# Cross attention's query and output projections as seven products of quarters instead of eight

## The chip, the cores and the metric

One core of a Trainium2 chip runs the whole program. The metric is device time in microseconds (us) of one launch. All data are fp32. TensorE (PE in the profile; PEld is its weight load) multiplies, VectorE (DVE), ScalarE (ACT) and GpSimd (POOL) work on elements, and SyncE (SP) issues every transfer. Each engine takes its instructions in the program's order; semaphores hold one back until what it needs is there.

## What is computed

One layer of an encoder over `ctx_1024` (2 x 77 x 512) and one of a decoder over `x` (2 x 2048 x 512), both with 16 heads of 32. The change touches the decoder's cross attention, the middle line, which reads the encoder's 77 rows:

```python
y = y + _mha(yn, yn, dec_sa_in_w, dec_sa_in_b, dec_sa_out_w, dec_sa_out_b, sb)
y = y + _mha(_ln(y, dec_n2_s, dec_n2_b), memory, dec_ca_in_w, dec_ca_in_b, dec_ca_out_w, dec_ca_out_b, cb)
h = _ln(y, dec_n3_s, dec_n3_b)
y = y + (jax.nn.relu(h @ dec_ff1_w.T + dec_ff1_b) @ dec_ff2_w.T + dec_ff2_b)
```

`_mha` projects queries, keys and values, adds a bias by relative position to the scaled scores, takes a softmax, weighs the values and projects the result.

## The kernel before

**Two halves.** The 4096 tokens of the decoder are eight blocks of 512 tokens, each of four tiles of 128. The first half of the program is the decoder's self-attention, as 128 units (block, group of four heads, tile of queries), 16 units to a block, with the encoder spread between them; the results go to DRAM as `y1`. Extra work hangs in lists by unit: `light[n]`, `jobs[n]`, `late[n]` run in this order at the start of unit n, `ahead[n]` just before (L1003 `slot`, L1463). The unit u is the first of a block. Every block computes, during the block before it, its norm (L277 `norm_stats`, whose power stands on POOL, L285; L288 `norm_center`, on VectorE), in units 6 to 9, where also the residual's bias is added on POOL (L266). Block 0's cross attention runs in the first half too (L833 `first_cross`).

**Sums of weights.** In blocks 2 and 6 of the first half, in units u, u + 2, u + 4 and u + 10, quarters of the feed-forward weights are loaded, combined on POOL (L1090 `w2_sums`, L1123 `w1_sums`; L1088 `minus` is the helper that all subtractions go through) and stored in DRAM.

**The second half** (from about 1756 us) is the feed-forward of blocks 0 to 7, with the cross attention of block x + 1 laid beside that of block x. The feed-forward's products are already done as seven products of quarters instead of eight, after Winograd: `ONE` and `TWO` (L1157, L1166) list for each of the seven the weights' part, the tokens' part, the chain (one of two accumulating banks) and the quarter of the result that the bank's content goes to after it. A block has 56 slots (L1362 `ff_slot`): 0 to 27 hold the first layer's products, four matmuls of 128 x 256 each (L1292 `first_product`, L1301); 28 to 55 the second layer's, seven products of four parts (L1321 `second_product`, L1330), three parts with eight matmuls of 128 x 128 and the fourth with four. Sums of tokens feed them:

- `sums_n` (L1223), all four on POOL in slot 0, 512 wide (L1088).
- `sums_h` (L1258), one product ahead, in slots 24 to 51: the half sums on VectorE (L1250 and L1088), the others on POOL (L1268, L1088) where the product's part is itself a sum, as it is in products 1 to 4, hence in slots 28 to 43.
- Evictions of second products: L1338 on ScalarE, L1339 and L1344 to L1346 on VectorE, and the addition to y on POOL (L1349).

Weights come as tiles of 256 KB through a ring of 16 (L1195 `w_ring`, L1198 `feed`), in the order in which the products take them.

**Cross attention** (L1384 `cross`): a generator that adds, ahead of each slot's own products, what `plan[slot]` lists.

- Norm n2 (L732 `norm_stages`): tile t has its statistics (VectorE, then a power and a product on POOL, L743 and L744) in slot t, its centering (ScalarE, L750) and the addition of a bias row to y (POOL, L751) in slot t + 2, its turning (four transposes on PE, L756, and four copies on ScalarE, L759) in slot t + 4.
- Queries (L763 `q_group`): four groups of features in slots 9 to 12, four matmuls of 128 x 512 each (L766), evicted on VectorE with bias and scale (L767).
- Attention per tile (L769 `attend_stages`), from slot 14, 21, 28 and 35: the scores (PE L781) with maximum and subtraction (VectorE L790, L791), the exponential (ScalarE L794), three slots later the row sums (VectorE L799, L800) and the division (POOL L805), then the turning of the probabilities (PE L811, ScalarE L812) after six, the values (PE L819, ScalarE L823) after nine, and the output (four matmuls of 128 x 512, L828, added to y on VectorE, L829) after eleven: slots 25, 32, 39 and 46. The first tile's scores stand one slot and its exponential, sums and division one slot or none earlier than this.
- Norm n3, whose turned result feeds the next block's first products: statistics, centering with addition, turning in slots 27, 29, 31 for tile 0 and 7 slots later for each further tile (48, 50, 52 for tile 3).

The side work uses four PSUM banks in turn (`bank`), the feed-forward the other four. The last block has nothing beside it.

Of the kernel before, what the change touches and what calls it, by code (L numbers as in the profile page):

```python
# [10 lines left out]
F32 = mybir.dt.float32  # L11
# [43 lines left out]
def tile_encoder_decoder(ctx: ExitStack, tc: tile.TileContext, ins, out):  # L55
# [5 lines left out]
    def wchunk(name, c0, n=D):  # L61

        return ins[name][:, c0 : c0 + n].rearrange("(c p) o -> p c o", p=P)
# [4 lines left out]
    ident = const.tile([P, P], F32, name="ident")  # L68
    make_identity(nc, ident)
    mhalf = const.tile([P, TB], F32, name="mhalf")  # L70
    nc.gpsimd.memset(mhalf, -0.5)
    vecs = const.tile([P, NVEC], F32, name="vecs")

# [84 lines left out]
    with (  # L158
# [573 lines left out]
        def norm_stages(y, n, row, place, done):  # L732

            keep = {}

            def stats():
                st = sm.tile([P, 6], F32, name="bnst", tag="bnst")
                mv = sm.tile([P, 2], F32, name="cmv", tag="cmv", bufs=4)
                rs = sm.tile([P, 3], F32, name="crs", tag="crs", bufs=4)
                nc.vector.bn_stats(st, y())  # L740
                nc.vector.bn_aggr(mv, st)
                nc.vector.tensor_scalar_add(rs[:, 0:1], mv[:, 1:2], EPS)
                nc.gpsimd.tensor_tensor(rs[:, 1:2], rs[:, 0:1], mhalf[:, 0:1], ALU.pow)  # L743
                nc.gpsimd.tensor_scalar(rs[:, 2:3], mv[:, 0:1], rs[:, 1:2], -1.0, ALU.mult, ALU.mult)  # L744
                keep.update(rs=rs)

            def center():
                xn = keep["xn"] = place()
                rs = keep["rs"]
                nc.scalar.activation(xn, y(), AF.Identity, bias=rs[:, 2:3], scale=rs[:, 1:2])  # L750
                nc.gpsimd.tensor_tensor(y(), y(), row, ALU.add)  # L751

            def turned():
                xn, pt, dst = keep["xn"], bank(), done()
                for c in range(NC):
                    nc.tensor.transpose(pt[:, ts(c, P)], xn[:, ts(c, P)], ident)  # L756
                for c in range(NC):
                    sc, bi = vec(f"dec_{n}_s", c), vec(f"dec_{n}_b", c)
                    nc.scalar.activation(dst[:, c, :], pt[:, ts(c, P)], AF.Identity, bias=bi, scale=sc)  # L759

            return stats, center, turned

        def q_group(o, w, nT, dst):  # L763
            mm = bank()
# [4 lines left out]
        def attend_stages(q, kTc, v, y, biased, pr, pts, place, w_o, bi=None):  # L769
# [58 lines left out]
                    nc.tensor.matmul(mm, oT[:, ts(c, P)], w_o[:, c, :], start=(c == 0), stop=(c == NC - 1))  # L828
                nc.vector.tensor_tensor(y(), mm, y(), ALU.add)  # L829

            return score, exp, sums, normalize, turned, times_v, out

        def first_cross():  # L833

# [40 lines left out]
            for t in range(TB):  # L875
                y = lambda t=t: ys[t]
                fs = norm_stages(
                    y, "n2", rows["dec_ca_out_b"], lambda: xn, lambda t=t: nT[:, :, ts(t, P)]
                )
                for k, f in enumerate(fs):  # L880
                    at(1 + t + k, f)
            for g in range(NC):
                at(7 + g, lambda g=g: q_group(g, wq[:, :, ts(g, P)], nT, qT[:, g, :]))
            for t in range(TB):
                y = lambda t=t: ys[t]
                fs = attend_stages(
                    lambda g, t=t: qT[:, g, ts(t, P)], kTc, vc, y, t < 2, prs[t % 2], pts, lambda: oT, wo
                )
# [3 lines left out]
                for k, f in enumerate(fs):  # L892
# [133 lines left out]
        w_q, vcs, qT = [], [], []  # L1026

        def big(i):
            return vflat[:, i * TB * D : (i + 1) * TB * D]
# [3 lines left out]
        def y_of(x, t):  # L1033
            return ys[x % 3][:, t, :]
# [6 lines left out]
        def early_loads():  # L1041
            nc.sync.dma_start(nTt, nT3_d)
            row_into(bv, "dec_ca_out_b")
            for o in range(2):
                w_q.append(small_w(o * P, "dec_ca_in_wT"))
            w_q.append(pts_all[:, 6, :].rearrange("p (c o) -> p c o", c=NC))

        def last_loads():
            t = sb.tile([P, MB], F32, name="q", tag="q", bufs=3)
            t = t.rearrange("p (c o) -> p c o", c=NC)  # L1050
            nc.sync.dma_start(t, wchunk("dec_ca_in_wT", (NC - 1) * P, P))
            w_q.append(t)
            for b in range(B):
                t = sb.tile([P, MB], F32, name="q", tag="q", bufs=3)
                nc.sync.dma_start(t[:S, :], cv_d[:, b, :])
                vcs.append(t)

        def late_loads():
            nc.sync.dma_start(w_q[2], wchunk("dec_ca_in_wT", 2 * P, P))
# [15 lines left out]

        w1_d = dram.tile([4, NC, P, D], F32, name="w1_d")
        w2_d = dram.tile([7, 7, P, D], F32, name="w2_d")
        free = pp[:, 3 * HC * MB : END - 3 * HC * MB]
        tens = free.rearrange("p (z q o) -> p z q o", z=8, q=2)
        ones = {  # L1080
# [55 lines left out]
        def w1_store(n):  # L1136
            nc.sync.dma_start(
                w1_d[:, n].rearrange("s p x -> p s x"), free[:, 4 * D :].rearrange("p (s x) -> p s x", s=4)
            )

        u = 2 * NU
        for c, k in enumerate((0, 2, 4, 10)):
            light[u + k + 2].append(lambda c=c: w2_store(c, 1))
# [36 lines left out]
        def w1_tile(name, n):  # L1180
# [3 lines left out]
            o = r * (DFF // 2) + n * TOK  # L1184
            return ins["dec_ff1_wT"][c * TOK : (c + 1) * TOK, o : o + TOK].rearrange("(c p) o -> p c o", p=P)

        def weight_tiles():
            for x in range(len(blocks)):
                for j, n in first_slots:
                    yield w1_tile(ONE[j][0], n)  # L1190
                for _, name, _, _, _ in TWO:
                    for k in range(7):
                        yield w2_d[ON_W2[name], k]
# [29 lines left out]
        def sums_n():  # L1223
            minus(gp, of_n("T1"), of_n("12"), of_n("11"))
            minus(gp, of_n("T2"), of_n("22"), of_n("T1"))
            minus(gp, of_n("T3"), of_n("22"), of_n("12"))
            minus(gp, of_n("T4"), of_n("21"), of_n("T2"))


        sets = [[high[:, (4 * a + k) * D : (4 * a + k + 1) * D] for k in range(4)] for a in range(2)]  # L1230
# [153 lines left out]
        def cross(x):  # L1384
# [162 lines left out]
```

## Time and profile before

| | us |
|---|---|
| median of three runs | 2870.43 |
| lowest and highest | 2868.46, 2870.47 |
| the profiled execution's span | 2868.2 |
| TensorE busy | 2821.6 |
| VectorE busy | 1930.3 |
| ScalarE busy | 1371.7 |
| POOL busy | 741.8 |

The profile has no other time of its own execution than the span; runs of this kernel lie up to 2.3 us above it. In the timeline a row merges neighbouring instructions of one kind: start, length from the first start to the last end, engine, line, operation, what is written and read, count, and in brackets the idle time ahead of it with what ended it. A matmul of the code stands as two instructions in the trace. Matmuls overlap, so their pace is read from start to start, not from one's length.

### The profile page before, as it was taken

Reading aid. Unit: us, or ns where it says so; the run is one execution under the profiler, and the core shown is the slowest. Engines: PE = TensorE matmul, PEld = TensorE weight load, DVE = VectorE, ACT = ScalarE, POOL = GpSimd, SP = SyncE. Lnnn points to the kernel's source line nnn. Section 1 sums busy time; section 2 is a strip of 40 time slices with the busy share of each in tenths; the row PEclk is TensorE's granted clock in tenths of the full one; section 3 lists DMA queues with packets and bytes.
Section 4 is the critical chain, followed back from the end, with each engine's and each line's share of the span. In section 5 each row is a group of like instructions: output and inputs, shape, how many; then the busy total and the mean of one; then the engine's idle time right before and its main releaser. Section 6 shows DMA issues by size and latency. Waiting matters only on the chain.

```text
span 2868.2 us, 64539 instructions
## 1 busy us (share of the span) xinstructions
PE 2821.6 (98%) x25782; PEld 2036.2 (71%) x25782; DVE 1930.3 (67%) x5422; ACT 1371.7 (48%) x2583; POOL 741.8 (26%) x637
## 2 busy tenths in 40 slices
PE   9899999999999999999999999999999999999998
PEld 5557666666666556666666677787878788888888
DVE  4767688778987668788878894555555555554545
ACT  3344455556666446565546665333333333333331
POOL 0100050200000201120100002272737373736355
PEclk9899999999999999999999999999999999999999
DMA  6413443401111512232301115464647464645365
GB/s 174 117 33 122 124 135 101 119 20 45 33 44 58 137 29 62 77 100 71 93 16 39 38 35 162 149 188 125 188 126 205 129 188 127 186 129 184 115 204 181
DMA packets 251773, 316.16 MB, mean 110 GB/s; under 512 B 29472, under 2 KB 142672, under 8 KB 251346
## 3 DMA queue, kind: packets, MB, share of 16 engines
q1 hardware_dynamic: 251474, 312.05, 36.7%
q8 instruction: 203, 3.33, 0.5%
q14 instruction: 96, 0.79, 0.1%
HBM read 273.07 MB, written 38.90 MB: 109 GB/s over the span
## 4 chain that ended last, share of the span: by engine, by line
PE 90%; DVE 3%; ACT 3%; POOL 2%; DMA 1%; issue 1%; SPq 0%; POOLq 0%; DVEq 0%; ACTq 0%
PE psum L425 17%; PE psum L1330 12%; PE psum L1301 11%; PE psum L371 11%; PE psum L442 9%; PE psum L828 4%; PE psum L766 4%; PE psum L215 4%; PE psum L239 4%; PE psum L251 4%; PE psum L226 3%; PE psum L811 2%; PE psum L781 1%; PE psum L819 1%; ACT pp L402 1%
## 5 line engine op out<-in xcount | busy, mean ns | idle before, releaser
L402 ACT ACTIVATE pp<-pp,nm 128x128 f32<-128x128 f32 (+15 forms) x512 | 611.9, 1201 | 263.2 <-DVE nm L397 262.9
L380 DVE TENSOR_SCALAR_CACHE_REDUCE pp<-psum 128x512 f32<-128x512 f32 (+3 forms) x1024 | 559.5, 591 | 62.1 <-PE psum L371 59.9
L425 PEld LDWEIGHTS psum<-ident,pp 128*128 128x128 f32 x4352 | 475.1, 142 | 110.5 <-DVE pp L380 50.8
L425 PE MATMUL psum<-ident,pp 128*128 128x128 f32 x4352 | 537.8, 278 | 8.5 <-DVE mx L387 3.8
L431 ACT COPY pts<-psum 128x512 f32<-128x512 f32 (+3 forms) x592 | 297.9, 575 | 470.9 <-PE psum L425 364.8
L429 DVE COPY pts<-psum 128x512 f32<-128x512 f32 (+2 forms) x544 | 329.9, 659 | 67.8 <-PE psum L425 67.5
L371 PE MATMUL psum<-kT,q 32*128 32x512 f32 (+3 forms) x2560 | 362.8, 578 | 5.9 <-ACT pts L431 3.3
L442 PEld LDWEIGHTS psum<-pts,vv 128*32 128x32 f32 x8704 | 227.3, 110 | 126.2 <-issue 117.3
L1330 PE MATMUL psum<-pp 128*128 128x128 f32 x2560 | 306.4, 276 | 1.9 <-POOL pp L1088 1.6
L1330 PEld LDWEIGHTS psum<-pp 128*128 128x128 f32 x2560 | 295.8, 192 | 17.4 <-issue 12.1
L442 PE MATMUL psum<-pts,vv 128*32 128x128 f32 x8704 | 280.9, 277 | 0.7 <-ACT pts L431 0.5
L1301 PE MATMUL psum<-vv,pp 128*128 128x256 f32 x1024 | 238.5, 381 | 0.0
L371 PEld LDWEIGHTS psum<-kT,q 32*128 32x128 f32 x2560 | 125.3, 184 | 143.3 <-issue 88.2
L1301 PEld LDWEIGHTS psum<-vv,pp 128*128 128x128 f32 x1024 | 189.8, 190 | 32.2 <-issue 8.4
L387 DVE CUSTOM_DVE_ANT_0 pp<-psum,bias 128x256 f32<-128x256 f32 (+1 forms) x512 | 196.0, 411 | 16.3 <-PE psum L371 16.3
L1088 POOL TENSOR_TENSOR pp<-pp 128x512 f32<-128x512 f32 x124 | 171.0, 1394 | 105.4 <-DMA pp<-in_dec_ff_wT_dram 91.2
L285 POOL TENSOR_TENSOR rstd<-rstd,mhalf 128x1 f32<-128x1 f32 x32 | 18.2, 570 | 662.8 <-DVE rstd L284 662.8
L1314 DVE TENSOR_TENSOR kT<-kT,psum 128x512 f32<-128x512 f32 x96 | 65.8, 686 | 170.3 <-PE psum L1301 96.9
L1317 ACT ACTIVATE kT<-kT,vecs 128x256 f32<-128x256 f32 x192 | 86.9, 500 | 192.0 <-DVE kT L1314 192.0
L1301 PE MATMUL psum<-nT,pp 128*128 128x256 f32 x768 | 173.4, 379 | 0.0
L1301 PEld LDWEIGHTS psum<-nT,pp 128*128 128x128 f32 x768 | 145.3, 190 | 28.6 <-issue 10.2
L805 POOL TENSOR_TENSOR oT<-oT,cri 128x1232 f32<-128x1232 f32 x28 | 67.7, 2419 | 346.2 <-DVE cri L800 346.2
(187 smaller groups left out, 3671.8 us busy)
## 6 DMA issues: line engine op xcount, KB each, us to landing
pp<-w_d SPq DMA_DIRECT2D x520, 256.0 KB, 3.0
pp<-in_dec_ff_wT_dram SPq DMA_DIRECT2D x112, 256.0 KB, 3.9
wqk<-in_dec_sa_in_wT_dram SPq DMA_DIRECT2D x64, 256.0 KB, 4.0
bias<-tzg SPq DMA_DIRECT2D x128, 128.0 KB, 3.8
wbig<-in_dec_sa_in_wT_dram SPq DMA_DIRECT2D x8, 1024.0 KB, 6.5
vv<-in_enc_ff_wT_dram SPq DMA_DIRECT2D x8, 1024.0 KB, 5.7
wbig<-in_dec_sa_out_wT_dram SPq DMA_DIRECT2D x8, 1024.0 KB, 6.4
vv<-y SPq DMA_DIRECT2D x32, 256.0 KB, 4.9
```

The source lines that it names most:

```text
L215: nc.tensor.matmul(mm, w[:, c, :], nTs[b, m][:, c, :], start=(c == 0), stop=(c == NC - 1))
L371: nc.tensor.matmul(banks[r][:, : kn * P], q[rows4(r), ts(t, P)], kT[rows4(r), g, k0 * P : (k0 + kn) * P], start=True, stop=True,)
L380: nc.vector.tensor_scalar(p[:, k0 * P : (k0 + far) * P], s[:, : far * P], 1.0, None, ALU.mult, ALU.max, accum_out=st["mx"][:, r, c : c + 1],)
L387: nc.vector.tensor_tensor_reduce(p[:, (i + 1) * P - w : (i + 1) * P], s[:, far * P : kn * P], biases[b, m, g][:, r, 2 * P - w :], 1.0, LOW ...
L402: nc.scalar.activation(p, p, AF.Exp, bias=nm, accum_out=to)
L425: nc.tensor.transpose(pt[:, ts(x, P)], state[n]["p"][r][:, ts(k, P)], ident)
L429: nc.vector.tensor_copy(pts[:, : len(load), :], pt[:, :w])
L431: nc.scalar.copy(pts[:, : len(load), :], pt[:, :w])
L442: nc.tensor.matmul(ot[rows4(r), t, :], vv[:, k, ts(g * HC + r, HD)], got.pop((n, k, r)), start=(k == 0), stop=(k == i),)
L1088: engine.tensor_tensor(out, a, b, ALU.subtract)
L1301: nc.tensor.matmul(mm[:, ts(f, TOK)], a[:, c, ts(f, P)], b[:, c, :], start=fresh and f == 0 and c == 0, stop=c == 1, skip_group_check=True,)
L1330: nc.tensor.matmul(psum[:, bank_i, ts(col, P)], lhs[:, c, :], w[:, c, :], start=fresh and k in (0, 3) and c == 0, stop=c == 3, skip_group_ ...
```

## The change

The query projection and, for pairs of tiles, the output projection become seven products of quarters each, with sums of weights made in the first half and streamed through the ring; the sums of tokens and some additions move. Both are done for the cross attentions of blocks 1 to 7; `first_cross` keeps its form (it uses the norm's new fourth stage).

- In units u + 7 of blocks 2 and 6 of the first half (u = 32 and 96), four loads and four POOL operations 512 wide make four weight sums, and a store in unit u + 8 puts them into DRAM.
- Query products: 0 and 1 in slot 9, 2 and 3 in slot 10, 4 and 5 in slot 11, 6 in slot 12, four matmuls of 128 x 256 each, on four token sums made on POOL in slots 8 and 9. First results of a quarter are evicted on ScalarE in two halves, later ones on VectorE.
- Output products: for tiles 0 and 1 in slots 31 to 33, for tiles 2 and 3 in slots 46 to 48, two matmuls of 128 x 256 each, on four sums made on VectorE, 256 wide, at the beginning of slots 31 and 46. Each product's bank is added to y on VectorE, 256 wide.
- Norm n2's addition to y goes from slot t + 2 to t + 11. Norm n3's statistics go to slots 35, 36, 49 and 50 for tiles 0 to 3, centering and addition two slots, turning four slots later.
- The four sums of `sums_n` go to slots 0, 1, 4 and 6, one each.

```diff
@@ norm_stages
                 nc.scalar.activation(xn, y(), AF.Identity, bias=rs[:, 2:3], scale=rs[:, 1:2])
+
+            def add():
                 nc.gpsimd.tensor_tensor(y(), y(), row, ALU.add)
...
-            return stats, center, turned
+            return stats, center, turned, add
@@ sums of weights
+        def wc_sums(name, turned):
+            z = free.rearrange("p (z k o) -> p z k o", z=8, k=2)
+            q = {}
+            for i, (r, c) in enumerate(((0, 0), (0, 1), (1, 0), (1, 1))):
+                nc.sync.dma_start(z[:, i], quarter(name, c, r) if turned else quarter(name, r, c))
+                q[r, c] = z[:, i]
+            s1, s2, s3, s4 = (z[:, 4 + i] for i in range(4))
+            if turned:
+                gp.tensor_tensor(s1, q[1, 0], q[1, 1], ALU.add)
+                minus(gp, s2, s1, q[0, 0])
...
+        for u, name, turned, dst in (
+            (2 * NU, "dec_ca_in_wT", True, wq_d), (6 * NU, "dec_ca_out_wT", False, wo_d)
+        ):
+            light[u + 7].append(lambda name=name, turned=turned: wc_sums(name, turned))
+            late[u + 8].append(lambda dst=dst: wc_store(dst))
@@ the ring's order
+        Q_SLOTS = {9: (0, 1), 10: (2, 3), 11: (4, 5), 12: (6,)}
+        O_SLOTS = {at + k: js for at in (31, 46) for k, js in enumerate(((0, 1), (2, 3), (4, 5, 6)))}
...
         def weight_tiles():
             for x in range(len(blocks)):
...
+                for n in range(per):
+                    if x + 1 < len(blocks):
+                        yield from cross_tiles(n)
@@ ff_slot
-            if n == 0:
-                sums_n()
+            if n in (0, 1, 4, 6):
+                sum_n(f"T{(0, 1, 4, 6).index(n) + 1}", of_n)
@@ cross
-                for k, f in zip((0, 2, 4), fs):
+                for k, f in zip((0, 2, 4, 11), fs):
                     plan[t + k].append(f)
-            for g in range(NC):
-                plan[9 + g].append(lambda g=g: q_group(g, w_q[g], nT2, qT[g // 2][:, g % 2, :]))
...
+            def q_product(j):
+                if j == 0:
+                    held["q"] = bank(), bank()
+                name, by, chain, fresh, to = ONE[j]
+                a, n, mm = next_w(2), of_n2(by), held["q"][chain]
+                for f in range(2):
+                    for c in range(2):
+                        nc.tensor.matmul(
+                            mm[:, ts(f, TOK)], a[:, c, ts(f, P)], n[:, c, :],
+                            start=fresh and f == 0 and c == 0, stop=c == 1, skip_group_check=True,
+                        )
+                r, c = int(to[0]) - 1, int(to[1]) - 1
+                got, dst = mm.rearrange("p (f n) -> p f n", f=2), qT[r][:, :, ts(c, TOK)]
+                if to in [p[4] for p in ONE[:j]]:
+                    nc.vector.scalar_tensor_tensor(dst, got, SCALE, dst, ALU.mult, ALU.add)
+                else:
+                    for f in range(2):
+                        nc.scalar.activation(
+                            dst[:, f, :], got[:, f, :], AF.Identity, bias=qbias[:, 2 * r + f : 2 * r + f + 1], scale=SCALE
+                        )
+
+            plan[8].append(lambda: [sum_n(n, of_n2) for n in ("T1", "T2")])
+            plan[9].append(lambda: [sum_n(n, of_n2) for n in ("T3", "T4")])
...
+            def sums_o(t):
+                s = {n: of_o(t, n) for n in ("S1", "S2", "S3", "S4", "11", "12", "21", "22")}
+                ve.tensor_tensor(s["S1"], s["21"], s["22"], ALU.add)
+                minus(ve, s["S2"], s["S1"], s["11"])
+                minus(ve, s["S3"], s["11"], s["21"])
+                minus(ve, s["S4"], s["12"], s["S2"])
+
+            def o_product(t, j):
+                if j == 0:
+                    held["out"] = bank(), bank()
+                name, by, chain, fresh, to = ONE[j]
+                a, mm = of_o(t, name), held["out"][chain][:, :TOK]
...
+                for c in range(2):
+                    nc.tensor.matmul(
+                        mm, a[:, ts(c, P)], w[:, c, :], start=fresh and c == 0, stop=c == 1, skip_group_check=True
+                    )
+                d = y_of(x, t + int(to[0]) - 1)[:, ts(int(to[1]) - 1, TOK)]
+                ve.tensor_tensor(d, d, mm, ALU.add)
+
+            for n, js in Q_SLOTS.items():
+                plan[n].append(lambda js=js: [q_product(j) for j in js])
+            for n, js in O_SLOTS.items():
+                t = 0 if n < 40 else 2
+                if 0 in js:
+                    plan[n].append(lambda t=t: sums_o(t))
+                plan[n].append(lambda t=t, js=js: [o_product(t, j) for j in js])
...
-                for k, f in zip((0, 2, 3, 3, 6, 9, 11) if t else (-1, 1, 2, 3, 6, 9, 11), fs):
+                for k, f in zip((0, 2, 3, 3, 6, 9) if t else (-1, 1, 2, 3, 6, 9), fs):
                     plan[at + k].append(f)
                 fs = norm_stages(y, "n3", bo, place("xt"), lambda t=t: nTt[:, :, ts(t, P)])
-                for k, f in zip((13, 15, 17), fs):
+                at = (35, 36, 49, 50)[t]
+                for k, f in zip((0, 2, 4, 2), fs):
                     plan[at + k].append(f)
```

More of the change, by code (lines that the diff above doesn't have):

```diff
@@ L70, in tile_encoder_decoder @@
     mhalf = const.tile([P, TB], F32, name="mhalf")
+    qbias = const.tile([P, NC], F32, name="qbias")
     nc.gpsimd.memset(mhalf, -0.5)
@@ L829, in out @@
                 nc.vector.tensor_tensor(y(), mm, y(), ALU.add)
-            return score, exp, sums, normalize, turned, times_v, out
+            return score, exp, sums, normalize, turned, times_v, out, keep
         def first_cross():
@@ L879, in first_cross @@
                 )
-                for k, f in enumerate(fs):
+                for k, f in zip((0, 1, 2, 1), fs):
                     at(1 + t + k, f)
@@ L1077, in tile_encoder_decoder @@
         w2_d = dram.tile([7, 7, P, D], F32, name="w2_d")
+        wq_d = dram.tile([4, P, D], F32, name="wq_d")
+        wo_d = dram.tile([4, P, D], F32, name="wo_d")
         free = pp[:, 3 * HC * MB : END - 3 * HC * MB]
@@ L1139, in w1_store, with quarter, wc_store @@
             )
+        def quarter(name, r, c):
+            return ins[name][r * TOK : (r + 1) * TOK, c * TOK : (c + 1) * TOK].rearrange("(c p) o -> p c o", p=P)
+        def wc_sums(name, turned):
[8 more added lines that the diff above has]
+                minus(gp, s2, s1, q[0, 0])
+                minus(gp, s3, q[0, 0], q[1, 0])
+                minus(gp, s4, q[0, 1], s2)
+            else:
+                minus(gp, s1, q[0, 1], q[0, 0])
+                minus(gp, s3, q[1, 1], q[0, 1])
+                minus(gp, s2, q[1, 1], s1)
+                minus(gp, s4, q[1, 0], s2)
+        def wc_store(dst):
+            nc.sync.dma_start(
+                dst.rearrange("s p x -> p s x"), free[:, 4 * D :].rearrange("p (s x) -> p s x", s=4)
+            )
[4 more added lines that the diff above has]
+            late[u + 8].append(lambda dst=dst: wc_store(dst))
         u = 2 * NU
@@ L1185, in w1_tile, with cross_tiles @@
             return ins["dec_ff1_wT"][c * TOK : (c + 1) * TOK, o : o + TOK].rearrange("(c p) o -> p c o", p=P)
+        Q_SLOTS = {9: (0, 1), 10: (2, 3), 11: (4, 5), 12: (6,)}
+        O_SLOTS = {at + k: js for at in (31, 46) for k, js in enumerate(((0, 1), (2, 3), (4, 5, 6)))}
+        def cross_tiles(n):
+            for j in Q_SLOTS.get(n, ()):
+                name = ONE[j][0]
+                yield wq_d[int(name[1]) - 1] if name[0] == "S" else quarter(
+                    "dec_ca_in_wT", int(name[1]) - 1, int(name[0]) - 1
+                )
+            for j in O_SLOTS.get(n, ()):
+                name = ONE[j][1]
+                if name[0] == "T":
+                    yield wo_d[int(name[1]) - 1]
         def weight_tiles():
             for x in range(len(blocks)):
[L1189 to L1193, printed above, removed]
+                for n in range(per):
+                    if x + 1 < len(blocks):
+                        yield from cross_tiles(n)
+                    if n < FIRST:
+                        j, f = first_slots[n]
+                        yield w1_tile(ONE[j][0], f)
+                    else:
+                        j, part = divmod(n - FIRST, 4)
+                        for k in range(2 * part, min(2 * part + 2, 7)):
+                            yield w2_d[ON_W2[TWO[j][1]], k]
         w_ring = [low[:, j % 4 * T + j // 4 * D : j % 4 * T + j // 4 * D + D] for j in range(16)]
@@ L1221, in of_n, with sum_n @@
             return nTt[:, 2 * r : 2 * r + 2, ts(c, TOK)]
[L1223 to L1227, printed above, removed]
+        T_OF = {"T1": ("12", "11"), "T2": ("22", "T1"), "T3": ("22", "12"), "T4": ("21", "T2")}
+        def sum_n(name, of):
+            minus(gp, of(name), *(of(a) for a in T_OF[name]))
         sets = [[high[:, (4 * a + k) * D : (4 * a + k + 1) * D] for k in range(4)] for a in range(2)]
```

37 lines of the change are left out of this document (28 added, 9 removed).

## The prediction

> **What bounds the kernel now.** The page first: its span and its engines.
>
> ```profile
> span 2868.2 us, 64539 instructions
> PE 2821.6 (98%) x25782; PEld 2036.2 (71%) x25782; DVE 1930.3 (67%) x5422; ACT 1371.7 (48%) x2583; POOL 741.8 (26%) x637
> ```
>
> TensorE (PE) is busy for 98%, so time is won by giving PE less to do, and lost wherever PE must wait. The shares hide stages, so next comes the view by windows, over slots 0 to 27, 28 to 43 and 44 to 55 of one feed-forward block (after the times: PE, PE weight load, VectorE, ScalarE, POOL; then granted clock, DMA share, GB/s).
>
> ```profile
> 2053.80:2130.80 77.00, 75.22 (x410) 57.23 (x408) 28.99 (x57) 35.01 (x73) 22.28 (x23) 1.00 0.41 117
> 2130.80:2172.20 41.40, 41.40 (x411) 36.36 (x411) 36.93 (x57) 13.83 (x28) 33.36 (x22) 1.00 0.64 193
> 2172.20:2196.40 24.20, 24.20 (x218) 22.09 (x218) 9.62 (x20) 5.80 (x14) 18.06 (x17) 1.00 0.72 226
> ```
>
> In the first stretch VectorE is busy 29.0 of 77 us and POOL 22.3: room. In the second VectorE is busy 36.9 of 41.4 us and POOL 33.4 while PE never pauses: three engines close to full. The clock is 1.00 in both. What the change puts into slots 28 to 43 has almost nowhere to hide. That decides the forecast.
>
> **Fewer columns on PE: 22.5 us won.** The PE timeline, and the rows of the two projections by line:
>
> ```profile
> 2120.37 3.60 PE L828 MATMUL psum<-wbig,xr 128*128 128x512 f32 x8
> 2123.80 1.89 PE L1301 MATMUL psum<-nT,pp 128*128 128x256 f32 x8
> 2125.53 1.89 PE L1301 MATMUL psum<-vv,pp 128*128 128x256 f32 x8
> ```
>
> ```profile
> L766 PE MATMUL psum<-pp,wqk x112: 592/592/593, 1788.4 to 2652.2; 128*128 128x512 f32 x112
> ```
>
> From start to start, eight instructions 512 wide take 3.43 us (2120.37 to 2123.80) and eight 256 wide 1.73. Each matmul of the code stands as two instructions here, so eight are one query group or one output tile (four matmuls); L766's two first weight tiles alone are 112, half of 7 blocks x 4 groups x 8 = 224. A block has four groups and four outputs: 8 x 3.43 = 27.4 us. After, seven query products of four matmuls (1.73 each) and twice seven output products of two (0.865 each): 24.2. The saving is 3.2 us a block, 22.5 in seven. Weight loads double in number, but the 256-wide row above already holds that pace, so they cost nothing more.
>
> **The stall at a block's start: 11.4 us won.** PE, POOL and ScalarE in slots 0 to 8:
>
> ```profile
> 2053.80 7.07 PE L1301 MATMUL psum<-nT,pp 128*128 128x256 f32 x32
> 2060.70 0.60 PE L756 MATMUL psum<-ident,xt 128*128 128x128 f32 x4
> 2061.14 1.89 PE L1301 MATMUL psum<-vv,pp 128*128 128x256 f32 x8
> 2064.12 0.66 PE L756 MATMUL psum<-ident,pts 128*128 128x128 f32 x4 [1.08 <-ACT pts L750]
> ...
> 2067.00 0.66 PE L756 MATMUL psum<-ident,xt 128*128 128x128 f32 x4 [0.50 <-ACT xt L750]
> ...
> 2069.58 0.66 PE L756 MATMUL psum<-ident,xt 128*128 128x128 f32 x4 [0.19 <-ACT xt L750]
> ```
>
> ```profile
> 2057.26 1.27 POOL L1088 TENSOR_TENSOR vv<-nT 128x512 f32<-128x512 f32 x1
> ...
> 2062.30 0.55 POOL L743 TENSOR_TENSOR crs<-crs,mhalf 128x1 f32<-128x1 f32 x1
> ```
>
> ```profile
> 2057.93 0.81 ACT L750 ACTIVATE xt<-vv,crs 128x512 f32<-128x512 f32 x1
> 2059.97 0.91 ACT L1317 ACTIVATE kT<-kT,vecs 128x256 f32<-128x256 f32 x2 [1.22 <-DVE kT L1314]
> ...
> 2064.77 1.48 ACT L759 ACTIVATE pp<-psum,vecs 128x128 f32<-128x128 f32 x4
> ...
> 2066.84 0.58 ACT L1311 COPY kT<-psum 128x512 f32<-128x512 f32 x1
> ```
>
> A turning and a slot take 0.44 + 1.73 = 2.17 us, but the second to fourth turning start 3.42, 2.88 and 2.58 us after the one before: 2.37 us lost, in six blocks (blocks 1 to 6; the first turns its tiles before its products run so). The four token sums (2057.26 to 2062.30) hold back the second tile's power on POOL, then the addition of L751 the later ones. Singly, the second power follows the first sum, near 2059.4, and the additions go to slots 11 to 14, where POOL has room. Late next is ScalarE: from 2059.97 it has two pairs of L1317, three centerings, two turnings' copies and a copy ahead of the fourth turning, 2 x 0.91 + 3 x 0.81 + 2 x 1.48 + 0.58 = 7.8 us, so 2067.8 against PE at 2060.70 + 3 x 2.17 = 2067.2. I leave 0.5 us of the stall (0 to 1.0): 1.9 x 6 = 11.4 won. The token sums still arrive in time: the order on POOL is power, T1, power, T2, so T2 ends near 2060.7 and is wanted at 2061.1. The new query sums (4 x 1.27, slots 8 and 9) are wanted from slot 10, one slot of products 2 x 1.73 + 1.73 = 5.2 us later: covered.
>
> **Slots 31 to 33: 2.3 us a block lost.** The output products now come in pairs of tiles, and each is added into y from its bank; products 0, 2, 4, 6 share one bank, 1, 3, 5 the other, so product 2 waits for the addition of product 0, and product 6 for that of 4. VectorE, in the program's order, has other work between these additions.
>
> ```profile
> 2135.72 1.89 DVE L1250 TENSOR_TENSOR pp<-kT 128x512 f32<-128x512 f32 x3
> ...
> 2139.21 1.42 DVE L799 TENSOR_REDUCE csu<-oT 128x16 f32<-128x1232 f32 x1
> ...
> 2140.84 0.36 DVE L1344 TENSOR_TENSOR oT<-psum,oT 128x256 f32<-128x256 f32 x1
> 2141.23 0.42 DVE L1345 TENSOR_TENSOR oT<-psum,oT 128x256 f32<-128x256 f32 x1
> ...
> 2143.52 0.69 DVE L829 TENSOR_TENSOR vv<-psum,vv 128x512 f32<-128x512 f32 x1 [1.66 <-PE psum L828]
> 2144.12 4.86 DVE L1088 TENSOR_TENSOR pp<-pp,kT 128x512 f32<-128x512 f32 x3
> ```
>
> A 512-wide sum takes 0.63 us where POOL idles (1.89 for three) and 1.62 where POOL adds too (4.86 for three). No row shows one 256 wide; half of these bounds it, 0.3 to 0.8, so the four new ones take 1.2 to 3.2. VectorE is free at 2139.2, 0.7 after slot 31 began on PE (2138.55, the row quoted below); product 0's addition (0.42) ends 2.3 to 4.3 after it, while PE wants the bank at 1.73 + 0.89 = 2.6. Wait 0 to 1.7; I take 0.8. Then come one addition, the reduce with its reciprocal (1.6, 2139.21 to 2140.84), three evictions (at most 0.42 each, 1.1), two additions, two 512-wide sums (1.3 to 3.2) and product 4's addition: 4 x 0.42 + 1.6 + 1.1 + 1.3 to 3.2 = 5.7 to 7.6 us. PE needs 2 x 1.73 for four products and 1.79 for one part of sixteen 128-wide instructions (24 take 2.81 from 2163.01 to 2165.82, below, 0.1 of it waited): 5.25. Wait 0.4 to 2.4; I take 1.5, near the upper end since the 1.62 row is from this very place. The second pair (slots 46 to 48) meets a light VectorE: 0.2. Slot 27: with the output of slot 25 (3.43) gone, PE reaches the turning of tile 1 earlier, and I take 0.1 for its wait on POOL.
>
> Here the Trainium skill, page "SBUF — State Buffer", section "Who interferes with whom", speaks against the change: a VectorE operation with two SBUF inputs and a POOL operation exclude each other for a whole instruction. The rows agree roughly: behind one another, 0.63 and POOL's 1.27 would be 1.9, and 1.62 was measured.
>
> **Slot 41: 5.2 us a block lost.** POOL, and PE beside it:
>
> ```profile
> 2151.42 1.00 POOL L743 TENSOR_TENSOR crs<-crs,mhalf 128x1 f32<-128x1 f32 x1
> 2152.52 0.27 POOL L744 TENSOR_SCALAR crs<-cmv,crs 128x1 f32<-128x1 f32 x1
> ...
> 2156.75 1.65 POOL L1349 TENSOR_TENSOR vv<-vv,oT 128x512 f32<-128x512 f32 x1 [1.50 <-DVE oT L1346]
> 2158.36 1.72 POOL L751 TENSOR_TENSOR vv<-vv,row_dec_sa_out_b 128x512 f32<-128x512 f32 x1
> ...
> 2163.07 2.70 POOL L805 TENSOR_TENSOR oT<-oT,cri 128x1232 f32<-128x1232 f32 x1
> ```
>
> ```profile
> 2138.55 0.60 PE L756 MATMUL psum<-ident,pts 128*128 128x128 f32 x4
> ...
> 2150.51 1.13 PE L781 MATMUL psum<-pts,bias 32*128 32x77 f32 x32
> ...
> 2159.57 3.60 PE L828 MATMUL psum<-wbig,xr 128*128 128x512 f32 x8
> 2163.01 2.84 PE L1330 MATMUL psum<-pp 128*128 128x128 f32 x24
> 2165.82 1.97 PE L811 MATMUL psum<-ident,oT 128*77 128x128 f32 x16
> ```
>
> POOL runs without a gap from 2156.75 to the end of L805 at 2165.77, and PE turns those probabilities at 2165.82: already just in time. The chain hangs on the scores of 2150.51, since VectorE must finish with them before the eviction that L1349 waits for: L1349 starts 6.2 us after them, L805 ends 9.0 later. The change moves two n3 stages into slots 35 to 40, so between L1349 and L805 POOL has one power more (0.82 to 1.27) and one L751 more (1.27 to 1.72): it ends 6.2 + 9.0 + 2.1 to 3.0 = 17.3 to 18.2 after the scores. PE has less in between: 15.3 minus the output of slot 39 (3.44) plus one more turning (0.44) minus the 0.1 it waited: 12.2. Wait 5.1 to 6.0; if POOL ran at the undisturbed 1.27 for 512 columns throughout (five operations by 0.4 less), about 3.5. I take 5.2. Slots 42 to 55 are light and catch up.
>
> **The rest.** Slots u+7 of blocks 2 and 6 of the first half get four loads and four POOL sums (5.1 us), with the next power on POOL behind them:
>
> ```profile
> 492.54 1.27 POOL L266 TENSOR_TENSOR xr<-xr,row_dec_sa_out_b 128x512 f32<-128x512 f32 x1
> 507.67 0.55 POOL L285 TENSOR_TENSOR rstd<-rstd,mhalf 128x1 f32<-128x1 f32 x1 [13.86 <-DVE rstd L284]
> ```
>
> ```profile
> pp<-in_dec_ff_wT_dram SPq DMA_DIRECT2D x112, 256.0 KB, 3.9
> ```
>
> With a landing of 3.9 the sums end in 9 of 13.9 us; four loads one behind another (15.6) would overrun by 7 each. I take 1 for both (0 to 14), near the single landing. Query evictions move to ScalarE (35 of 77 us) and VectorE (29): nothing. Fifteen more tiles of 256 KB a block go through SP's queue; at a DMA share of 0.41 to 0.64 and a ring of 16 ahead, nothing; if that cover went, one landing of 3.9 a block, 27.
>
> **Sum.** Per block 2.3 + 0.2 + 0.1 + 5.2 = 7.8, times 7 = 54.6. -22.5 - 11.4 + 54.6 + 1 = +21.7 on the profiled span of 2868.2, which lies 2.2 below the median of the runs, 2870.4: **2892**.
>
> **Rivals.** (a) *Faster*: VectorE and POOL hide it all, the queues' slack (4.5 and 8 us of 41) taking the new work; -22.5 - 11.4 = 2837 with no stall. It decides below a stall of 33.9 / 7 = 4.8 us a block. For: VectorE's L829 goes, it idles 1.66 ahead of it. Against: L805 ending 0.05 us ahead of L811. 2837 to 2862: 0.17. (b) Only one of the two places stalls (2.3 or 5.2): 2854 to 2874, with a short stall at the other to 2880: 0.18. (c) Worse: each of the four new sums waits out a POOL operation of 1.27, 5.1 us in place of the 2 taken, and two more in the second pair: 3 to 5 more a block, 2908 to 2930: 0.12. The Trainium skill's rule of exclusion, taken strictly, gives this case. (d) 256-wide products don't run at 0.216 a piece with new weights each: nothing is won on PE, 2915; the rows above show the pace: 0.02.
>
> **How the numbers follow.** The forecast, 2880 to 2908, has 0.51. Bounds of the terms: stalls 3.8 to 10.7 a block (27 to 75) give 2861 to 2926; I draw the range to 2850 to 2914, half of (a) and most of (c) left out. A measurement tells about 0.2% (5.7 us). Slower by more: the forecast, (c), (d) and a third of (b), 0.71; within: half of (b), 0.09; faster: (a) and the rest, 0.20.
>
> **What would show it.** Right: at slot 41 L811 waits 4 to 6 us for POOL L805 in seven blocks; output products 2 and 6 wait for VectorE; L756's waits on L750 at block starts nearly gone; a block near 145 us instead of 142.6 (2053.80 to 2196.40). Wrong: L811 without a wait, or PE in the second stretch without gaps, and blocks of 138.

## The result, and the profile after

The changed kernel took **2914.41 us**, the median of 4 runs (2914.07 to 2915.84), against 2869.81 for the kernel before (4 runs, 2868.46 to 2870.47): a ratio of 1.0156, 95% interval 1.0144 to 1.0168. The forecast had the direction and the two places, but half the size: +21.7 us against +44.6.

The page of the changed kernel, its span and its engines:

```profile
span 2912.3 us, 65731 instructions
PE 2818.4 (97%) x26118; PEld 2114.6 (73%) x26118; DVE 1969.7 (68%) x5542; ACT 1394.5 (48%) x2639; POOL 780.2 (27%) x673
```

PE's busy time fell by only 3.2 us though 22.5 us of columns are gone, so something takes longer per instruction. PE also waits. These are its waits in the second half, summed by what released them (total us, times, longest):

```profile
PE psum L814 <- POOL oT L808: 31.8, 8, 4.3
PE psum L1510 <- DVE vv L1514: 12.8, 7, 1.8
PE psum L1510 <- issue: 8.3, 5, 1.7
PE psum L1383 <- DVE pp L1091: 4.3, 7, 0.6
```

L814, L1383, L808 and L759 are L811, L1330, L805 and L756 of before; L1510 is an output product, L1514 its addition to y. Seven of L814's eight waits are those of slot 41, 4.3 each. The same three stretches as in the prediction, for one block of the changed kernel (the third, as there):

```profile
2066.60:2136.47 69.87, 69.87 (x427) 60.36 (x425) 27.19 (x52) 38.13 (x81) 26.84 (x25) 1.00 0.53 154
2136.47:2187.87 51.40, 44.66 (x421) 41.39 (x421) 39.77 (x66) 13.99 (x28) 35.74 (x26) 0.93 0.59 177
2187.87:2214.72 26.85, 26.85 (x238) 25.79 (x237) 14.22 (x33) 5.91 (x14) 15.17 (x15) 1.00 0.77 246
```

Slots 0 to 27 fell from 77.00 us to 69.87: the query products are narrower, one tile's output product (3.43) has left, and so has the stall. Slots 28 to 43 grew from 41.40 to 51.40, with 6.7 us in which PE is idle and a granted clock of 0.93. Slots 44 to 55 grew from 24.20 to 26.85, since the second pair's products (14 x 0.43 = 6.06 us) stand there in place of one tile's (3.43). The block went from 142.60 to 148.12.

The start of that block on PE, in which the stall was:

```profile
2066.60 7.07 PE L1354 MATMUL psum<-nT,pp 128*128 128x256 f32 x32
2073.51 0.60 PE L759 MATMUL psum<-ident,xt 128*128 128x128 f32 x4
...
2075.67 0.60 PE L759 MATMUL psum<-ident,pts 128*128 128x128 f32 x4
...
2077.84 0.60 PE L759 MATMUL psum<-ident,xt 128*128 128x128 f32 x4
...
2080.13 0.66 PE L759 MATMUL psum<-ident,xt 128*128 128x128 f32 x4
```

The turnings follow one another at 2.16, 2.17 and 2.29 us: the 2.37 us a block are gone but for 0.1. Slots 31 to 41 on PE instead:

```profile
2144.19 1.89 PE L1510 MATMUL psum<-wbig,xr 128*128 128x256 f32 x8
2145.92 1.05 PE L1383 MATMUL psum<-pp,kT 128*128 128x128 f32 x8
2148.80 3.66 PE L1510 MATMUL psum<-pp,wqk 128*128 128x256 f32 x8 [1.83 <-DVE vv L1514]
...
2174.56 1.16 PE L1383 MATMUL psum<-pp 128*128 128x128 f32 x8 [0.62 <-DVE pp L1091]
2180.01 3.46 PE L814 MATMUL psum<-ident,oT 128*77 128x128 f32 x16 [4.30 <-POOL oT L808]
```

Three waits: product 2 (2148.80) for product 0's addition, the half sum of slot 40, and the probabilities of slot 41. And two rows run at half pace: products 2 and 3, eight instructions, in 3.66 us for 1.89, and the sixteen instructions of the turning in 3.46 for 1.97 in the kernel before. The clock says why, in windows around the second row:

```profile
2176.30:2179.60 3.30, 0.00 (x0) 0.00 (x0) 3.30 (x2) 0.00 (x0) 3.30 (x2) 1.00 0.34 79
2179.70:2183.10 3.40, 3.09 (x15) 3.09 (x16) 0.80 (x1) 1.31 (x3) 3.40 (x4) 0.50 0.00 0
2183.20:2186.50 3.30, 3.30 (x32) 3.30 (x31) 1.09 (x2) 1.18 (x3) 3.22 (x3) 1.00 0.32 82
```

After the pause the granted clock is 0.50 for 3.4 us. The changed kernel has nine such stretches in the second half, 44.4 us in all: one at each of the seven waits of slot 41, and one behind product 2 in two of the seven blocks. The kernel before has none there (the last 3 us of both programs, behind the last matmul, apart).

### The profile page after: what moved, and what is told of

Same layout as the page of the kernel before. It is cut to its first block, busy times and chain, and to the rows that moved or that the text cites. A ratio compares the mean times of both kernels' runs of the same rounds, so it can differ in the third digit from the quotient of the medians.

```text
span 2912.3 us, 65731 instructions
## 1 busy us (share of the span) xinstructions
PE 2818.4 (97%) x26118; PEld 2114.6 (73%) x26118; DVE 1969.7 (68%) x5542; ACT 1394.5 (48%) x2639; POOL 780.2 (27%) x673
## 4 chain that ended last, share of the span: by engine, by line
PE 86%; DVE 7%; issue 3%; POOL 2%; ACT 1%; DMA 0%; SPq 0%; POOLq 0%; DVEq 0%; ACTq 0%
PE psum L426 17%; PE psum L1354 13%; PE psum L372 11%; PE psum L443 8%; PE psum L1383 8%; PE psum L216 4%; PE psum L240 4%; PE psum L252 4%; PE psum L227 3%; PE psum L1468 3%; PE psum L1510 3%; PE psum L814 2%; PE psum L784 1%; ACT pp L403 1%; PE psum L544 1%
## 5 line engine op out<-in xcount | busy, mean ns | idle before, releaser
L1383 PE MATMUL psum<-pp 128*128 128x128 f32 x2560 | 313.8, 278 | 6.2 <-DVE pp L1091 4.6
L1383 PEld LDWEIGHTS psum<-pp 128*128 128x128 f32 x2560 | 302.0, 194 | 14.6 <-DVE pp L1091 6.1
L1091 POOL TENSOR_TENSOR pp<-pp 128x512 f32<-128x512 f32 x131 | 185.3, 1432 | 112.8 <-DVE vv L243 62.0
L286 POOL TENSOR_TENSOR rstd<-rstd,mhalf 128x1 f32<-128x1 f32 x32 | 18.2, 569 | 646.8 <-DVE rstd L285 646.8
L1391 ACT COPY oT<-psum 128x128 f32<-128x128 f32 x56 | 14.9, 266 | 264.1 <-PE psum L1383 264.1
```

The source lines that it names most:

```text
L1091: engine.tensor_tensor(out, a, b, ALU.subtract)
L1383: nc.tensor.matmul(psum[:, bank_i, ts(col, P)], lhs[:, c, :], w[:, c, :], start=fresh and k in (0, 3) and c == 0, stop=c == 3, skip_group_ ...
```

## The experiments

Theory: VectorE and POOL are the limit of slots 28 to 48. Pairing the output products moves n3's work on tiles 0 and 1 and the new sums into these slots, PE waits for both engines, and each long wait costs a stretch at half clock on top. Rivals: the narrow query products or their weight traffic cost the time (e2, e7); one badly placed step does, and moving it gives the gain back (e3, e4, e9). Each run's ratio is to the kernel before, run beside it.

**e1_moves_only: the kernel before with the token sums one by one and n2's additions later.**

```
-            if n == 0:
-                sums_n()
+            if n in (0, 1, 4, 6):
+                sum_n(f"T{(0, 1, 4, 6).index(n) + 1}", of_n)
...
-                for k, f in zip((0, 2, 4), fs):
+                for k, f in zip((0, 2, 4, 11), fs):
```

> The kernel before with the moves alone: the four token sums in slots 0, 1, 4 and 6, norm n2's additions nine slots later; both projections as eight products, norm n3 untouched. Theory: L756's waits on L750 at six block starts (2.3 us each) go and nothing follows them, about 2857 us (2853 to 2862). Rival: the wait only moves on to ScalarE or to the next slots, 2866 to 2871.

Measured: 2855.33 us, ratio 0.9946 (0.9931 to 0.9961). Six blocks became shorter by 2.27 us each (142.57 to 140.30), 13.6 in all. The moves alone make a faster kernel.

**e2_q_only: the changed kernel with the output projections and n3 as they were before.**

```
-        O_SLOTS = {at + k: js for at in (31, 46) for k, js in enumerate(((0, 1), (2, 3), (4, 5, 6)))}
+        O_SLOTS = {}
...
-                for k, f in zip((0, 2, 3, 3, 6, 9) if t else (-1, 1, 2, 3, 6, 9), fs):
+                for k, f in zip((0, 2, 3, 3, 6, 9, 11) if t else (-1, 1, 2, 3, 6, 9, 11), fs):
...
-                at = (35, 36, 49, 50)[t]
-                for k, f in zip((0, 2, 4, 2), fs):
+                for k, f in zip((13, 15, 17, 15), fs):
```

> The changed kernel with its output projection, its second weight sums and norm n3 as before; queries in seven products, moves kept. Theory: the loss belongs to what stands in slots 31 to 41, so this gains half the columns (11.3 us) and the starts (13): about 2846 us (2841 to 2852), no waits at L1510's place or at the turning of slot 41. Rival: streaming tiles and narrow products cost time wherever they stand; then half of the loss shows, about 2890.

Measured: 2845.68 us, ratio 0.9913 (0.9898 to 0.9928). It beats both kernels, and is the version to keep. One block by the same windows:

```profile
2048.10:2121.24 73.14, 73.14 (x435) 61.97 (x433) 28.07 (x56) 38.37 (x81) 27.16 (x27) 1.00 0.50 149
2121.24:2162.96 41.72, 41.39 (x409) 36.34 (x409) 36.95 (x57) 13.89 (x28) 33.35 (x22) 1.00 0.63 192
2162.96:2187.14 24.18, 24.18 (x218) 22.07 (x217) 9.62 (x20) 5.80 (x14) 18.07 (x17) 1.00 0.70 222
```

Slots 28 to 55 are about what they were before (41.40 and 24.20), at full clock. So query products and moves cost nothing there; the loss belongs to the output half of the change, that is, the paired output products together with n3's new places.

**e5_one_add and e6_three_adds: the kernel before with one, or three, more POOL additions ahead of slot 41's probabilities.** Their results are used by nobody. The edit of e5, where e6 has `range(3)`:

```
+                if t == 3:
+                    for _ in range(1):
+                        plan[at + 3].append(lambda: gp.tensor_tensor(of_n("T1"), of_n("T2"), of_n("T3"), ALU.add))
```

> The kernel before with one more POOL addition (512 wide, into a token sum that is no longer read) ahead of the division for tile 3 in slot 38. Theory: POOL's chain from the scores of slot 35 to that division is the bound of the stretch, so the addition's 1.3 to 1.7 us show in each of seven blocks, with no half clock: 2879 to 2883 us. Rival: POOL's 8 idle us in 41 take it: 2869 to 2873.

> The same with three such additions. Theory: a pause of 4 to 5 us at slot 41 in seven blocks, as in the changed kernel, and behind it the granted clock falls to a half, which costs about 1.5 more: 2905 to 2918 us. Rival: a pause costs only its own length: 2900 to 2904; or POOL's idle time takes half: under 2890.

Measured: 2877.71 us, 1.0026 (1.0017 to 1.0035), and 2922.06, 1.0177 (1.0162 to 1.0193). PE at slot 41, with one addition and with three:

```profile
2454.74 1.97 PE L811 MATMUL psum<-ident,oT 128*77 128x128 f32 x16 [1.20 <-POOL oT L805]
```

```profile
2485.13 3.69 PE L811 MATMUL psum<-ident,oT 128*77 128x128 f32 x16 [4.66 <-POOL oT L805]
```

POOL had nothing to spare there: one addition makes a wait of 1.2 us where there was none, and three one of 4.66. Seven waits of 4.66 are 32.6 of the 51.4 us; behind each, the turnings run at half clock (here 3.69 for 1.97), as they don't behind the short wait, and from their start to the end of the forty matmul instructions after them 18.4 us more went by in the seven blocks: together 51.0. POOL's work alone makes the drop too, without any part of the change. The first run ended 1.3 us below its expectation, the second 4 above.

**e8_fill_41: the changed kernel with 18 idle matmuls on PE in slot 41**, ahead of the turning, written to a bank that nobody reads.

```
+            def fill(k):
+                idle = bank()
+                count["bank"] -= 1
+                for _ in range(k):
+                    nc.tensor.matmul(idle[:, :P], ident, ident, start=True, stop=True)
+
+            plan[41].append(lambda: fill(18))
```

> The changed kernel with 18 idle matmuls (128 wide, about 4 us) ahead of the turning in slot 41, in the time in which PE waits for POOL. Theory: the pause shrinks to under 1 us, the clock stays whole behind it, the sixteen transposes take 1.8 instead of 3.3 us, and each of seven blocks is 1.4 to 2 us shorter: 2900 to 2906. Rival: those transposes are slow because ScalarE is slow to empty their banks; then nothing changes, 2912 to 2916.

Measured: 2906.02 us, ratio 1.0126 (1.0111 to 1.0141). PE at slot 41:

```profile
2470.08 4.18 PE L1503 MATMUL psum<-ident 128*128 128x128 f32 x36
2474.55 1.97 PE L814 MATMUL psum<-ident,oT 128*77 128x128 f32 x16 [0.29 <-POOL oT L808]
```

The probabilities come as late as in the changed kernel, but the turnings take 1.97 again, and the second half has no stretch at half clock left (44.4 us in the changed kernel). Work for nothing wins 8.4 us; the second half's 1157.7 us become 1147.7. The waits ahead of product 2, 1.83 us as before, dropped the clock in two blocks of the changed kernel and in none here, though nothing was done about them: behind a pause of that length the drop comes in some blocks and runs and not in others.

**e3_n3_late: n3 of tiles 0 and 1 in slots 41 and 42**, behind the probabilities.

```
-                at = (35, 36, 49, 50)[t]
+                at = (41, 42, 49, 50)[t]
```

> The changed kernel with norm n3 of tiles 0 and 1 six slots later (statistics in 41 and 42). Theory: ahead of the division for tile 3 POOL loses one power and two additions and VectorE one set of statistics, so the wait at slot 41 falls from 4.5 + 0.8 us to about 1.5 to 2 and the half clock behind it goes (1.5 us): 2876 to 2888. Rival: the wait is there only because PE lost the output projection of slot 39; then it stays, 2910 to 2916.

Measured: 2922.58 us, ratio 1.018 (1.0165 to 1.0195): 35 to 47 us more than expected.

```profile
2480.09 1.16 PE L1383 MATMUL psum<-pp 128*128 128x128 f32 x8 [1.35 <-DVE pp L1091]
2482.20 3.55 PE L814 MATMUL psum<-ident,oT 128*77 128x128 f32 x16 [0.95 <-POOL oT L808]
...
2501.73 2.70 PE L1510 MATMUL psum<-pp,wqk 128*128 128x256 f32 x8 [2.26 <-DVE vv L1514]
```

The long wait at slot 41 fell from 4.30 to 0.95, so n3's place is the cause of most of it. But the half sum is later (1.35 for 0.62), and the second pair's product 2 in slot 47, which did not wait in the changed kernel, now waits 2.26, and 2.3 to 3.1 over the blocks. The turnings still run at half clock in this block and two others, and the clock drops behind the new wait in all seven blocks. The waits of PE sum to 57 us, as in the changed kernel, but the second half has thirteen stretches at half clock, 51.2 us.

**e9_adds_later: only n3's additions of tiles 0 and 1 to slots 45 and 47**, its powers left.

```
-                for k, f in zip((0, 2, 4, 2), fs):
+                for k, f in zip((0, 2, 4, (10, 11, 2, 2)[t]), fs):
```

> The changed kernel with two POOL instructions a block moved: the additions of norm n3 for tiles 0 and 1 (L754) from slots 37 and 38, ahead of the division for tile 3, to slots 45 and 47. Theory: POOL's chain is shorter by their 1.3 and 1.7 us, the wait at slot 41 falls from 4.5 to about 1.5, too short for the half clock (1.4 more): about 4.4 a block, 2880 to 2890 us; the waits for VectorE at L1510 (2.0 and 1.8) stay. Rival: VectorE's half sums hold POOL's sum up anyway (the row before the division waits 0.6 for VectorE already); then half of it, 2895 to 2906.

Measured: 2904.99 us, ratio 1.0122 (1.0105 to 1.0139).

```profile
2471.15 1.97 PE L814 MATMUL psum<-ident,oT 128*77 128x128 f32 x16 [0.95 <-POOL oT L808]
...
2488.16 3.57 PE L1510 MATMUL psum<-pp,wqk 128*128 128x256 f32 x8 [2.28 <-DVE vv L1514]
```

Slot 41 is nearly cured, at full clock; the two additions, now beside the second pair's sums, make a new wait at slot 47, and there the clock drops in four of the seven blocks, this one among them. On VectorE, the last two of the four sums of slot 46 show why:

```profile
2484.88 1.48 DVE L1091 TENSOR_TENSOR wqk<-xr 128x256 f32<-128x256 f32 x1
2486.29 1.48 DVE L1091 TENSOR_TENSOR wqk<-xr,wqk 128x256 f32<-128x256 f32 x1
```

In the changed kernel these two take 0.42 each, with POOL idle; here POOL adds beside all four, which take 1.33 to 1.48. 9.4 us, a fifth of the loss, came back where 24 to 34 were expected. The rival had the size (2895 to 2906), but not the cause: the wait at slot 41 did go.

**e4_o_two_slots: products 2 to 6 of the first pair one behind another in slot 32.**

```
-        O_SLOTS = {at + k: js for at in (31, 46) for k, js in enumerate(((0, 1), (2, 3), (4, 5, 6)))}
+        O_SLOTS = {31: (0, 1), 32: (2, 3, 4, 5, 6), 46: (0, 1), 47: (2, 3), 48: (4, 5, 6)}
```

> The changed kernel with output products 2 to 6 of the first pair all in slot 32 instead of 32 and 33, so that no half sums stand between their additions on VectorE. Theory: product 6 waits for the addition of product 4 behind two 512-wide sums; that wait (1.8 us in a block) goes or falls under 0.5, the first one (2.0) stays: 2900 to 2906. Rival: the additions themselves are late because VectorE is; then both waits stay, 2912 to 2916.

Measured: 2917.12 us, ratio 1.0161 (1.0144 to 1.0178); a gain was expected, none came.

```profile
2452.15 1.99 PE L1510 MATMUL psum<-pp,wqk 128*128 128x256 f32 x8 [1.83 <-DVE vv L1514]
2455.57 1.13 PE L1510 MATMUL psum<-pp,wqk 128*128 128x256 f32 x4 [1.43 <-DVE vv L1514]
```

The wait of product 6 became one of product 4, 1.43 us: the reduce and three evictions stand on VectorE ahead of product 2's addition, and moving the products on PE doesn't move these.

**e7_q_and_second_pair: the queries and the outputs of tiles 2 and 3 in sevens, tiles 0 and 1 as before.** Tile 3's turning goes to slot 43, n3 of tiles 0 and 1 to slots 27 and 34.

```
+        O_SLOTS = {46: (0, 1), 47: (2, 3), 48: (4, 5, 6)}
...
+                if t == 3:
+                    offs = (0, 2, 3, 3, 8, 10)
...
+                at = (27, 34, 49, 50)[t]
```

> Queries in seven products and the outputs of tiles 2 and 3 too (slots 46 to 48, norm n3 of these in 49 and 50); tiles 0 and 1 as before; the probabilities of tile 3 are turned two slots later, in 43, so that POOL has time. Theory: POOL and VectorE are the bound of slots 28 to 43, so taking tile 2's output (3.4 us of PE) out of slot 39 only makes PE wait for POOL's sums there: 2862 to 2885, worse than the queries alone. Rival: with the turning put off, nothing waits and the columns saved count: 2838 to 2842.

Measured: 2873.45 us, ratio 1.0012 (1.0002 to 1.0021). It gives away all that e2 wins:

```profile
2449.89 6.61 PE L1383 MATMUL psum<-pp 128*128 128x128 f32 x40 [1.86 <-DVE pp L1091]
2456.34 1.91 PE L814 MATMUL psum<-ident,oT 128*77 128x128 f32 x16
```

The probabilities are in time now (no wait at 2456.34), and a half sum on VectorE is late instead, by 1.86 us in every block. In three of the seven blocks, this one among them, the clock drops behind that wait: the forty instructions take 6.61 us, for 4.63 at full clock in the kernel before. An output half alone, without the query half, was not tried.

## Why the prediction was wrong in size

On the profiled spans: forecast +21.7, measured 2912.3 - 2868.2 = +44.1. The result lies above the 2880 to 2908 of the forecast and just above the 2914 to which the range was drawn. Two steps failed: the term for slots 31 to 33, 2.3 us a block, was too small by 1.7, 12 us in all; and the clock behind the waits, which the sum put at nothing, took 14.1. Of the four signs named in advance, three came; the block near 145 us was 148.0 to 150.0.

- **Fewer columns, 22.5 won: right.** In e2 slots 0 to 27, which hold half of this saving and the start's gain, fell by 3.86 us a block, where 1.61 + 2.37 = 3.98 were to be had.
- **The stall at a block's start, 11.4 won: right, a little small.** Turnings at a pace of 2.2 us, and e1's six blocks, give 13.6.
- **Slots 31 to 33, 2.3 us a block lost: this step failed.** Product 2 was given 0.8, with 1.7 at most, and waited 1.83 by its row, 1.99 by the delay of its start; product 6 was given 1.5 and cost 1.8 plus 0.2: 4.0 us, 12 more over seven blocks than the term. In the blocks where product 6 waits, the profile names "issue" (five times 1.7); in the other two, products 2 and 3 ran at half clock instead (the 3.66 row), which uses the same time. What failed inside is the bound on the new sums, "half of" the 512-wide ones: 1.2 to 3.2 us for the four, where they took 3.5. VectorE and POOL in slots 31 and 32:

```profile
2144.86 1.48 DVE L1494 TENSOR_TENSOR wqk<-xr 128x256 f32<-128x256 f32 x1
2146.38 1.37 DVE L1091 TENSOR_TENSOR wqk<-wqk,xr 128x256 f32<-128x256 f32 x1
2147.67 0.41 DVE L1091 TENSOR_TENSOR wqk<-xr 128x256 f32<-128x256 f32 x1
2148.00 0.41 DVE L1091 TENSOR_TENSOR wqk<-xr,wqk 128x256 f32<-128x256 f32 x1
2148.34 0.94 DVE L1514 TENSOR_TENSOR vv<-vv,psum 128x256 f32<-128x256 f32 x2
```

```profile
2144.46 3.00 POOL L1091 TENSOR_TENSOR pp<-pp 128x512 f32<-128x512 f32 x2
```

  While POOL adds (to 2147.46) a 256-wide sum takes 1.48 and 1.37 us, nearly as long as a 512-wide one there (1.62 in the prediction's row); once it is idle, 0.41. All seven blocks show the same four lengths, and e9 makes the second pair's sums long by putting POOL's additions beside them. Width has little say: each sum seems to wait out a POOL operation. The Trainium skill, page "SBUF — State Buffer", section "Who interferes with whom", has this exclusion, and here it bears more than I gave it; but POOL's two took 3.00 us where alone they take 2.54, so POOL is slowed a little too. That these sums are what delays product 2's bank is read from the rows; no run took them alone away.
- **Second pair 0.2 and slot 27 0.1:** the second pair did not wait. At slot 27 six blocks lost 0.1 as forecast; the fourth lost 1.8, the eighth wait of L814. There alone VectorE adds the bias by position to the scores of tiles 0 and 1 (L791, four operations of 0.47 us for each tile), so the row sums and POOL's division come later; the kernel before has the same additions and no wait, with the output product of slot 25 still ahead of the turning.
- **Slot 41, 5.2 us a block lost: right**, 0.78 at the half sum and 4.46 at the probabilities, 5.24 by the delay of the starts. POOL ran without a gap as reckoned, here its first and last row:

```profile
2168.38 1.29 POOL L1402 TENSOR_TENSOR vv<-vv,oT 128x512 f32<-128x512 f32 x1 [4.74 <-DVE oT L1399]
...
2177.27 2.69 POOL L808 TENSOR_TENSOR oT<-oT,cri 128x1232 f32<-128x1232 f32 x1
```

  It ended 17.6 us after the scores of 2162.33; 17.3 to 18.2 were forecast.
- **The clock behind these waits: no step had it.** The sixteen instructions of the turning of slot 41 took 3.2 to 3.5 us instead of 1.8, and where the drop lasted 6.83 us the forty behind them ran slower too: 14.1 us over the seven blocks, from the turning's start to the end of those forty, against the kernel before. e8 took the drops away, and this stretch takes in it just what it takes in the kernel before; it won 10.0 in the second half and not 14.1, since the second pair's product 2 then waits for VectorE's addition (0.33 us by its row) and the slots there last 0.6 us longer in each block. e6 shows the same drop in the kernel before. I read "1.00 in both" as a fact of the kernel, where it is one of a PE that never pauses.
- **The rest, 1 us for u + 7: nothing.** The four sums end at 502.6, the next power is at 507.6. The fifteen more tiles a block cost nothing to be seen: no wait of PE in the second half names a transfer. POOL in unit u + 7:

```profile
498.85 3.76 POOL L1091 TENSOR_TENSOR pp<-pp 128x512 f32<-128x512 f32 x3
507.64 0.55 POOL L286 TENSOR_TENSOR rstd<-rstd,mhalf 128x1 f32<-128x1 f32 x1 [5.03 <-DVE rstd L285]
```

Measured terms: -22.5 - 13.6 + 4.0 x 7 + 5.24 x 7 + 14.1 + 1.8 = +44.5 for the second half, where the block starts show +46.3 (1111.4 to 1157.7). The first half came out 2.2 us shorter; over all kernels here it varies from 1754.5 to 1759.4, so I take that for the run's and not the change's, without having tested it; the kernel before has a stretch at half clock at 1500 us that the changed kernel has not. Of the rivals, (c) had the size, 2908 to 2930, and in part the cause: two of the first pair's four sums waited out a POOL operation, but one of the second pair's, without a wait on PE.

## What to carry to other kernels

Read a stage's room engine by engine before moving work into it: the output half's 11 of the 22.5 us of fewer columns were bought with work for two engines that were already full there, and each step that was moved away (e3, e4, e9, e7) made another one late. Split a change by where its work lands: the half with room (e2) won 25 us, the other lost 69 on top of it. And price a wait on PE twice, for itself and for the clock behind it; where the wait can't go, idle matmuls in it were cheaper here than the drop (e8).

## What the runs showed of the hardware

- **Pauses and the clock.** How often the granted clock fell to 0.50 at a pause of PE, by the idle time of its row:

| idle, us | where | dropped |
|---|---|---|
| 1.2 to 1.4 | slot 41 in e5, product 4 in e4 | 0 of 14 |
| 1.7 | product 6 (changed kernel, e3, e8, e9), slot 27 of the fourth block (these and e4) | 0 of 27 |
| 1.8, in two places of e3 1.9 and 2.2 | product 2 (changed kernel, e3, e4, e8, e9) | 6 of 35 |
| 1.86 | the half sum in e7 | 3 of 7 |
| 2.3 | slot 47 in e9 | 4 of 7 |
| 2.3 to 3.1 | slot 47 in e3 | 7 of 7 |
| 4.3 to 4.8 | slot 41 (changed kernel, e4, e6) | 21 of 21 |

  In e3 two pauses of 1.35 and 0.95 us, 2.1 us from one start to the other, did it in three of seven. The drop halves the clock for 3.41 or 6.83 us. The Trainium skill, page "TensorE: Matmul & The Clock Gate", section "Part 1: The HAM clock gate (the "warmup" mystery)", tells of free-running windows of some 3.4 us, and of half the clock after at least one idle one. The length of the drops, once or twice 3.41 us, agrees. The condition doesn't quite: a pause of 1.83 us can't fill such a window and dropped the clock now and then all the same, so a window that is idle for a part of it must count. Which part, these runs only bound.
- **A VectorE sum beside POOL costs POOL's length, not its own width:** 256 wide 1.33 to 1.48 us (the changed kernel, e9), alone 0.41; the 512-wide rows of the prediction are 1.62 and 0.63.
